# The first four slots of a per-sample matrix product with a residual, done with one row per partition

## Chip, cores and metric

The kernel runs on one core of a Trainium2 chip. The metric is the time of one execution on the device in microseconds (us), as the median of several runs.

## The reference

Each of 128 samples x[b] (128 rows c, 1024 columns t, float32) is multiplied by one of eight 128 x 128 matrices, which a list of subjects chooses, and added to itself:

```
w   = weights[subjects]                    # (128, 128, 128), subjects in 0..7
out = x + einsum("bct,bcd->bdt", x, w)     # x, out: (128, 128, 1024) float32
```

64 MB are read and 64 MB written. The residual costs no step of its own, since the kernel adds the identity to each matrix and multiplies once.

## The kernel before

**Slots.** A slot is four samples (Q = 4) and there are NT = 32 of them. The input buffer `x_in` holds IN = 4 slots, the output buffer `x_out` OUT = 8. A slot is 2 MiB each way. The two pairs of a slot (P = 2) have an accumulator each in PSUM, `ps[0]` and `ps[1]`, of four banks of 512 columns.

**Layout.** `load(k, p)` (L144) brings the two samples of pair p as one transfer of 1 MiB: sample h lies in partitions 64h to 64h+63, and each partition holds two neighbouring rows of it, 8 KB in one piece. `store` (L156) writes in the same way, 8 KB a run, 2 MiB a slot; the last twelve slots are stored in pairs of 4 MiB. With two rows in a partition a product of one sample has 64 partitions, and its 128 terms are two accumulated steps. `multiply` (L187) therefore issues 32 products of 64x64 by 512 columns for a slot, which TensorE runs four side by side; a float32 product is two instructions of TensorE.

**Matrices.** The matrices land in `w_raw` as they are, row c in partition c (L248). For the layout above row c has to stand in partition c/2, in both halves. Four products with the selection matrix `pick` move the rows (L296, into `ps[0]`), and two copies named `sort` write them in order to `w_all` (L231): half r = 1 on ScalarE (L305), half r = 0 on VectorE (L337). From `w_all`, `place` (L175) makes a slot's four matrices on VectorE: it picks the matrix by a subject read into a register, adds the identity `same`, and writes it to `ws[u]`, u alternating between slots.

**Order on the engines.** The order is written out by hand, and semaphores join the engines.

- ScalarE first issues the transfers of pair (0, 0), of the matrices, and of the other seven pairs (L247 to L290). Then it does its `sort`, and from then on for each slot `take` (L236): four copies `swap` (L225) move `ps[1]`, whose halves come out exchanged, to `x_out`. After each it waits for `s_eaten` and issues the two loads of the slot four further on.
- TensorE does idle products of zeros (IDLE = 6, L259), moves the rows (L296), and then runs `multiply` for one slot after another. A slot's product waits for `s_go` (its matrices are placed), `s_ready` (its input has landed) and `s_free` (the accumulator's half has been copied out).
- VectorE computes the subjects' indices, does its `sort`, waits for both sorts (`s_sort`), and places slots 0 and 1. Then for each slot it copies `ps[0]` to `x_out` in two halves of 1024 columns (L219), and places the matrices of the slot two further on. The first placing reports the slot to the store (`s_added[0]`), the second frees its input (`s_eaten`), the fourth gives `s_go`.
- GpSimd makes `pick` and `same`, and hands on landings (`s_ready`) and room in `x_out` (`s_room`, after a store has landed) in the order of the slots.
- SyncE issues a slot's store once VectorE and ScalarE have both reported it (L329).

`w_raw`, `pick`, `zeros` and the index scratch lie in the parts of `x_out` that belong to slots 6 and 7.

Of the kernel before, what the change touches and what calls it, by code (L numbers as in the profile page):

```python
# [27 lines left out]
ALU = mybir.AluOpType  # L28


H = 2

P = 2

R = 2

N = 512

IN = 4

OUT = 8
# [3 lines left out]

DMA = 16

IDLE = 6

ROWS = 8  # L50

ALIGN = 4096
QUEUES = {mybir.EngineType.SP: "qSPDynamicHW", mybir.EngineType.Activation: "qActDynamicHW"}
# [2 lines left out]
def transfer(nc, engine, out, in_):  # L56

    later, nc._always_lower_symbolic_ap = nc._always_lower_symbolic_ap, False  # L60
    ins, outs = engine.lower_ap_dma(in_), engine.lower_ap_dma(out)
    nc._always_lower_symbolic_ap = later
    return engine.add_instruction(
        mybir.InstDMACopy(
            name=nc.get_next_instruction_name(),
            engine=engine.engine,
            ins=ins,
            outs=outs,
            mode="Copy",
            cce_op=ALU.bypass,  # L70
            queue=QUEUES[engine.engine],
        )
    )
# [3 lines left out]
def kernel(  # L77
# [7 lines left out]
    nc = tc.nc  # L85
    B, C, T = x.shape
# [15 lines left out]
    if room:  # L102
# [4 lines left out]
    ws += [[sbuf(f"w{u}{p}", C, 1, R * D) for p in range(P)] for u in range(1, 2)]  # L107
    w_raw = x_out[:, (OUT * P - 1) * SIZE : (OUT * P - 1) * SIZE + S * D]
    pick = x_out[:, (OUT * P - 1) * SIZE + S * D :].rearrange("c (r p) -> c r p", p=C)[:, :R]
    zeros = x_out[:, (OUT * P - 2) * SIZE : (OUT * P - 2) * SIZE + N]  # L110
    given, near, wrap = (
        x_out[:1, (OUT * P - 3) * SIZE + k * B : (OUT * P - 3) * SIZE + (k + 1) * B].bitcast(I32)
        for k in range(3)
# [8 lines left out]
    s_zeros = tc.alloc_semaphore("s_zeros")  # L122
    s_same = tc.alloc_semaphore("s_same")
    s_pick = tc.alloc_semaphore("s_pick")
    s_picked = tc.alloc_semaphore("s_picked")
    s_sort = tc.alloc_semaphore("s_sort")
    s_ready = tc.alloc_semaphore("s_ready")
# [16 lines left out]
    def load(k, p, turn=None):  # L144
# [8 lines left out]
            x[bass.ds(first, H)].rearrange("h (b r) t -> (h b) (r t)", r=ROWS),  # L153
        ).then_inc(s_in[k % IN], DMA)

    def store(i, n):  # L156
        at = i % OUT * P * SIZE
        return transfer(
            nc,
            nc.sync,  # L160
            out[i * Q : (i + n) * Q].rearrange("(g h) (a r) t -> (h a) g (r t)", h=H, r=R),
            x_out[:, at : at + n * P * SIZE].rearrange("a (o f) -> a o f", o=1),
        )

# [10 lines left out]
    def place(u, subject):  # L175
        return [
            nc.vector.tensor_tensor(  # L177
                ws[u][p][h * A : (h + 1) * A],
                w_all[h * A : (h + 1) * A, bass.ds(subject[p * H + h], 1), :],
                same[h * A : (h + 1) * A],  # L180
                ALU.add,
            )
            for p in range(P)
            for h in range(H)
        ]

    def multiply(i):  # L187
        nc.tensor.wait_ge(s_go, 1).then_inc(s_go, -1)
# [28 lines left out]
    def copy(slot, half):  # L217
# [2 lines left out]
            x_out[:, bass.ds(at, T)], ps[0][:, banks].rearrange("d b n -> d (b n)")  # L220
        )

    def swap(slot, half, h):
        at, banks = half_of(slot, half)
        return nc.scalar.copy(  # L225
            x_out[h * A : (h + 1) * A, bass.ds(at + SIZE, T)],
            ps[1][(1 - h) * A : (2 - h) * A, banks].rearrange("d b n -> d (b n)"),
        )

    def sort(engine, r):  # L230
        engine(  # L231
            w_all.rearrange("c s (r e a) -> c r s e a", r=R, e=R)[:, r],
            ps[0][:, r * R : (r + 1) * R].rearrange("c g (s a e) -> c (g s) e a", a=A, e=R),
        ).then_inc(s_sort, 1)

    def take(i):  # L236
# [7 lines left out]

    with tc.tile_critical():  # L245

        load(0, 0)  # L247
        transfer(  # L248
            nc,
            nc.scalar,  # L250
            w_raw.rearrange("c (s d) -> c s d", s=S),
            weights.rearrange("s c d -> c s d"),
        ).then_inc(s_wall, DMA)
        nc.sync.dma_start(given, subjects.rearrange("(o b) -> o b", o=1)).then_inc(s_given, DMA)

        nc.vector.memset(zeros, 0.0).then_inc(s_zeros, 1)  # L256
        nc.tensor.wait_ge(s_zeros, 1)
        for _ in range(IDLE):
            nc.tensor.matmul(ps[P - 1][:, BANKS - 1], zeros[:, :D], zeros, start=True, stop=True)  # L259
        nc.vector.memset(index[:, B:], 0).then_inc(s_index, 1)  # L260

        nc.gpsimd.wait_ge(s_zeros, 1)
        nc.gpsimd.affine_select(  # L263
            pick.rearrange("c r (h b) -> c r h b", h=H),
            zeros[:, : R * C].rearrange("c (r h b) -> c r h b", r=R, h=H),
            [[-1, R], [0, H], [-R, A]],
            ALU.not_equal,
            1.0,
            base=0,
            channel_multiplier=1,  # L270
        ).then_inc(s_pick, 1)
# [12 lines left out]
        for p in range(P):  # L284
            nc.gpsimd.wait_ge(s_same, H).then_inc(s_room[p], OUT)

        for k in range(IN):
            for p in range(P):
                if (k, p) != (0, 0):
                    load(k, p)  # L290

        nc.tensor.wait_ge(s_pick, 1)
        nc.tensor.wait_ge(s_wall, DMA)
        for r in range(R):
            for g in range(S * D // N):
                nc.tensor.matmul(  # L296
                    ps[0][:, r * R + g],
                    pick[:, r],
                    w_raw[:, g * N : (g + 1) * N],
                    start=True,  # L300
                    stop=True,
                ).then_inc(s_picked, 1)

        nc.scalar.wait_ge(s_picked, S * D // N * R)
        sort(nc.scalar.copy, 1)  # L305
        with nc.scalar.Fori(0, NT // IN - 1) as turn:
            for k in range(IN):
                take((turn * IN + k) % OUT)
                nc.scalar.wait_ge(s_eaten, 1).then_inc(s_eaten, -1)
                for p in range(P):  # L310
                    load(IN + k, p, turn)
        for i in range(NT - IN, NT):
            take(i)

        nc.vector.wait_ge(s_given, DMA)
        nc.vector.tensor_scalar(near, given, -S, S - 1, ALU.max, ALU.min).then_inc(s_index, 1)  # L316
        nc.vector.wait_ge(s_index, 2)
        nc.vector.tensor_scalar(wrap, near, 0, S, ALU.is_lt, ALU.mult).then_inc(s_index, 1)  # L318
        nc.vector.wait_ge(s_index, 3)
        nc.vector.tensor_tensor(index[:, :B], near, wrap, ALU.add).then_inc(s_index, 1)  # L320

        for i in range(NT):
            if i - OUT in stored:
# [3 lines left out]
            nc.gpsimd.wait_ge(s_in[i % IN], DMA * P * (i // IN + 1)).then_inc(s_ready, 1)  # L327
# [12 lines left out]
        for u in range(2):  # L340
            placed = place(u, subject[u * Q : (u + 1) * Q])
            placed[0].then_inc(s_free[0], 1)
            placed[1].then_inc(s_free[1], 2)
            placed[-1].then_inc(s_go, 1)
        with nc.vector.Fori(0, NT // 2) as turn:  # L345
            for u in range(2):
                subject = subjects_of(bass.ds(turn * (2 * Q) + (u + 2) * Q, Q))
                slot = (turn * 2 + u) % OUT
                nc.vector.wait_ge(s_room[0], 1).then_inc(s_room[0], -1)
                for half in range(2):  # L350
                    nc.vector.wait_ge(s_product[0], H).then_inc(s_product[0], -H)  # L351
                    copied = copy(slot, half).then_inc(s_free[0], 1)
                placed = place(u, subject)
                placed[0].then_inc(s_added[0], 1)
                placed[1].then_inc(s_eaten, 1)
                placed[-1].then_inc(s_go, 1)
        with nc.tensor.Fori(0, NT // IN):
            for i in range(IN):
                multiply(i)

# [39 lines left out]
```

## Time and profile before

| | |
|---|---|
| median of 3 runs | 332.59 us (331.64 to 333.23) |
| profiled execution, whole time | 332.71 us |
| its span, first to last instruction | 330.9 us |
| moved by DMA | 134.81 MB, mean 407 GB/s over the span |
| TensorE, products | 255.5 us busy (77%) |
| VectorE | 138.0 us busy (42%) |
| ScalarE | 137.2 us busy (41%) |
| GpSimd | 1.6 us busy |
| mean granted TensorE clock | 0.928 |

The span is that of one profiled execution, and 1.8 us of its whole time lie around it. A busy share is a mean over the whole span. Where the work has stages with different limits, the rows by slices and stretches say more; in them a DMA packet is counted in the stretch in which it starts.

### The profile page before, as it was taken

The page shows a single profiled execution, that of the slowest core. Times are in us where ns is not written, and L with a number is a line of the kernel's source. Part 1 is how long each engine was busy: PE and PEld are TensorE (multiplying, and loading weights), DVE is VectorE, ACT ScalarE, POOL GpSimd, SP SyncE. Part 2 cuts the span into 40 slices and gives each one's busy share as a digit, 9 for nine tenths or more (in the row PEclk, how much of TensorE's full clock was granted, in tenths as well). Part 3 has the DMA queues.
Part 4 walks back from the last instruction along what each step waited for, and adds up shares of the span by engine and source line. Part 5 has one row for each costly group of instructions (what it writes and reads, how often), then busy time and mean ns, then how long its engine had stood idle before and what let it go on. Part 6 is the DMA issues. An engine that isn't in the chain of part 4 may idle for free. (4 is left out here: it accounts for less than half of the span.)

```text
span 330.9 us, 5722 instructions
## 1 busy us (share of the span) xinstructions
PE 255.5 (77%) x2068; PEld 93.3 (28%) x2068; DVE 138.0 (42%) x207; ACT 137.2 (41%) x162; POOL 1.6 (0%) x7
## 2 busy tenths in 40 slices
PE   7598888888888888888875897759887736999300
PEld 3243333333333333333222332213332302333100
DVE  1325555555444555555524255143555140444400
ACT  1105555555555555555525355153555050555500
POOL 1000000000000000000000000000000000000000
PEclk9979999999999999999979899798999775999955
DMA  7984999999999999999999999999999999999991
GB/s 277 428 372 129 431 421 416 436 432 426 442 418 434 436 424 434 444 428 426 430 442 402 434 424 435 428 428 430 432 450 424 430 432 436 428 408 432 436 440 48
DMA packets 7863, 134.81 MB, mean 407 GB/s; under 512 B 1457, under 2 KB 2482, under 8 KB 2482
## 3 DMA queue, kind: packets, MB, share of 16 engines
q10 hardware_dynamic: 4112, 67.64, 48.4%
q1 hardware_dynamic: 3746, 67.11, 47.5%
q8 instruction: 2, 0.03, 0.0%
q14 instruction: 3, 0.02, 0.0%
HBM read 67.63 MB, written 67.11 MB: 407 GB/s over the span
## 5 line engine op out<-in xcount | busy, mean ns | idle before, releaser
L202 PE MATMUL ps<-x_in,w 64*64 64x512 f32 x2048 | 244.2, 619 | 51.8 <-PEq L193 49.0
L225 ACT COPY x_out<-ps 64x1024 f32 (+1 forms) x128 | 128.8, 1007 | 161.9 <-ACTq L240 159.5
L202 PEld LDWEIGHTS ps<-x_in,w 64*64 64x64 f32 x2048 | 88.6, 138 | 207.3 <-issue 207.3
L219 DVE COPY x_out<-ps 128x1024 f32 x64 | 78.4, 1224 | 158.8 <-DVEq L351 158.8
L177 DVE TENSOR_TENSOR w<-w_all,same 64x256 f32<-64x256 f32 x136 | 57.1, 420 | 3.7
L259 PE MATMUL ps<-x_out 128*128 128x512 f32 x12 | 7.9, 825 | 1.7 <-DVE x_out L256 1.7
L243 ACT COPY mark<-same 1x1 f32 (+1 forms) x32 | 6.1, 190 | 0.8
L231 DVE COPY w_all<-ps 128x1024 f32<-128x1024 f32 x1 | 1.2, 1224 | 10.0 <-PE ps L296 10.0
L259 PEld LDWEIGHTS ps<-x_out 128*128 128x128 f32 x12 | 3.1, 270 | 5.6 <-issue 4.0
L231 ACT ACT_TABLE_LOAD x1 | 1.3, 1283 | 6.8 <-issue 6.8
L296 PE MATMUL ps<-x_out 128*128 128x512 f32 x8 | 3.6, 592 | 0.0
L231 ACT COPY w_all<-ps 128x1024 f32<-128x1024 f32 x1 | 1.0, 1012 | 4.9 <-PE ps L296 4.9
L296 PEld LDWEIGHTS ps<-x_out 128*128 128x128 f32 x8 | 1.5, 190 | 1.9 <-issue 1.9
L256 DVE MEMSET x_out<- 128x512 f32 x1 | 0.5, 485 | 1.0 <-SPq L245 1.0
L275 POOL TENSOR_SCALAR_AFFINE_SELECT same<-same 128x256 f32<-128x256 f32 x1 | 0.5, 529 | 0.1
L275 POOL TENSOR_SCALAR_AFFINE_SELECT same<-x_out 128x256 f32<-128x256 f32 x1 | 0.5, 479 | 0.0
L316 DVE TENSOR_SCALAR x_out<-x_out 1x128 int32<-1x128 int32 x1 | 0.2, 215 | 0.6 <-DMA x_out<-in_itok_B_dram 0.6
L263 POOL TENSOR_SCALAR_AFFINE_SELECT x_out<-x_out 128x256 f32<-128x256 f32 x1 | 0.4, 422 | 1.4 <-DVE x_out L256 1.4
L318 DVE TENSOR_SCALAR x_out<-x_out 1x128 int32<-1x128 int32 x1 | 0.3, 324 | 0.0
L320 DVE CUSTOM_DVE_ANT_0 index<-x_out 1x256 uint16<-1x256 uint16 x1 | 0.3, 279 | 0.0
L387 POOL MEMSET const-bfloat16-1.0<- 128x1 bf16 x1 | 0.1, 101 | 0.0
L387 POOL MEMSET const-uint8-127<- 128x1 uint8 x1 | 0.1, 101 | 0.0
(4 smaller groups left out, 0.3 us busy)
## 6 DMA issues: line engine op xcount, KB each, us to landing
x_in<-in_x_dram ACTq DMA_DIRECT2D x64, 1024.0 KB, 12.0
out_dram<-x_out SPq DMA_DIRECT2D x20, 2048.0 KB, 54.9
out_dram<-x_out SPq DMA_DIRECT2D x6, 4096.0 KB, 45.7
x_out<-in_L_cond_weights_dram ACTq DMA_DIRECT2D x1, 512.0 KB, 6.1
x_out<-in_itok_B_dram SPq DMA_DIRECT2D x1, 0.5 KB
```

The lines of the kernel that those rows point to most:

```text
L177: nc.vector.tensor_tensor(ws[u][p][h * A : (h + 1) * A], w_all[h * A : (h + 1) * A, bass.ds(subject[p * H + h], 1), :], same[h * A : (h + ...
L202: mm = nc.tensor.matmul(ps[p][cols, bank], ws[i % 2][p][rows, 0, r * D + e * A : r * D + (e + 1) * A], x_in[rows, at : at + N], start=r == ...
L219: return nc.vector.tensor_copy(x_out[:, bass.ds(at, T)], ps[0][:, banks].rearrange("d b n -> d (b n)"))
L225: return nc.scalar.copy(x_out[h * A : (h + 1) * A, bass.ds(at + SIZE, T)], ps[1][(1 - h) * A : (2 - h) * A, banks].rearrange("d b n -> d ( ...
L231: engine(w_all.rearrange("c s (r e a) -> c r s e a", r=R, e=R)[:, r], ps[0][:, r * R : (r + 1) * R].rearrange("c g (s a e) -> c (g s) e a" ...
L243: nc.scalar.copy(mark[:, bass.ds(slot, 1)], same[:1, 0, :1]).then_inc(s_added[1], 1)
L256: nc.vector.memset(zeros, 0.0).then_inc(s_zeros, 1)
L259: nc.tensor.matmul(ps[P - 1][:, BANKS - 1], zeros[:, :D], zeros, start=True, stop=True)
L263: nc.gpsimd.affine_select(pick.rearrange("c r (h b) -> c r h b", h=H), zeros[:, : R * C].rearrange("c (r h b) -> c r h b", r=R, h=H), [[-1 ...
L275: nc.gpsimd.affine_select(same[:, 0, :], same[:, 0, :] if h else zeros[:, : R * D], [[2 * C, R], [-2 * C, R], [-1, A]], ALU.not_equal, 1.0 ...
L296: nc.tensor.matmul(ps[0][:, r * R + g], pick[:, r], w_raw[:, g * N : (g + 1) * N], start=True, stop=True,).then_inc(s_picked, 1)
L318: nc.vector.tensor_scalar(wrap, near, 0, S, ALU.is_lt, ALU.mult).then_inc(s_index, 1)
```

## The change

Slots 0 to 3 (FIRST = 4) use another layout. `load_rows` brings one sample a transfer (512 KiB, sixteen transfers for the four slots) with row c in partition c, 4 KB in one piece, and the store of these slots writes rows of 4 KB. `place_rows` adds an identity `eye` (made on GpSimd ahead of `pick`) to a matrix as it landed in `w_raw`, 128 x 128. `multiply_rows` issues eight products of 128x128 by 512 columns for a slot, without accumulation, four into each accumulator, and reports each accumulator when its four are done. `copy_rows` on VectorE copies both accumulators, 2048 columns each, so that ScalarE has no part in these slots. Slots 4 to 31 go as before.

The rows are still moved for the later slots, ahead of slot 0, but into `ps[1]` instead of `ps[0]`. VectorE places slot 0 before its `sort`, and slot 1 after both sorts, with which `ps[1]` becomes free. Of the idle products three are left.

```diff
-IDLE = 6
+IDLE = 3
+FIRST = 4
...
+    def load_rows(i, q):
+        at = (i % IN * Q + q) * T
+        transfer(
+            nc,
+            nc.scalar,
+            x_in[:, at : at + T],
+            x[i * Q + q].rearrange("(b r) t -> b (r t)", r=C // 32),
+        ).then_inc(s_in[i % IN], DMA)
...
     def store(i, n):
         at = i % OUT * P * SIZE
+        if i < FIRST:
+            there = out[i * Q : (i + n) * Q].rearrange("g d t -> d g t")
+        else:
+            there = out[i * Q : (i + n) * Q].rearrange("(g h) (a r) t -> (h a) g (r t)", h=H, r=R)
...
+    def place_rows(u, subject):
+        return [
+            nc.vector.tensor_tensor(
+                ws[u][q // H][:, :, q % H * D : (q % H + 1) * D],
+                w_nat[:, bass.ds(subject[q], 1), :],
+                eye,
+                ALU.add,
+            )
+            for q in range(Q)
+        ]
+
+    def multiply_rows(slot, u):
+        nc.tensor.wait_ge(s_go, 1).then_inc(s_go, -1)
+        nc.tensor.wait_ge(s_ready, 1).then_inc(s_ready, -1)
+        for p in range(P):
+            nc.tensor.wait_ge(s_free[p], 1).then_inc(s_free[p], -1)
+            for bank in range(BANKS):
+                h, t = divmod(bank * N, T)
+                mm = nc.tensor.matmul(
+                    ps[p][:, bank],
+                    ws[u][p][:, 0, h * D : (h + 1) * D],
+                    x_in[:, bass.ds(slot * (Q * T) + ((p * H + h) * T + t), N)],
+                    start=True,
+                    stop=True,
+                )
+            mm.then_inc(s_product[p], 1)
...
+    def copy_rows(i, p):
+        at = i % OUT * P * SIZE + p * SIZE
+        return nc.vector.tensor_copy(
+            x_out[:, at : at + SIZE], ps[p].rearrange("d b n -> d (b n)")
+        )
...
-            ps[0][:, r * R : (r + 1) * R].rearrange("c g (s a e) -> c (g s) e a", a=A, e=R),
+            ps[1][:, r * R : (r + 1) * R].rearrange("c g (s a e) -> c (g s) e a", a=A, e=R),
         ).then_inc(s_sort, 1)
...
-        load(0, 0)
+        for q in range(H):
+            load_rows(0, q)
...
-        for k in range(IN):
-            for p in range(P):
-                if (k, p) != (0, 0):
-                    load(k, p)
+        for q in range(H, FIRST * Q):
+            load_rows(q // Q, q % Q)
...
         sort(nc.scalar.copy, 1)
-        with nc.scalar.Fori(0, NT // IN - 1) as turn:
+        for k in range(FIRST):
+            nc.scalar.wait_ge(s_eaten, 1).then_inc(s_eaten, -1)
+            for p in range(P):
+                load(FIRST + k, p)
+        with nc.scalar.Fori(0, (NT - FIRST) // IN - 1) as turn:
...
         for i, n in stores[:-1]:
-            for p in range(P):
-                nc.sync.wait_ge(s_added[p], i + n)
+            nc.sync.wait_ge(s_added[0], i + n)
+            if i >= FIRST:
+                nc.sync.wait_ge(s_added[1], i + n - FIRST)
...
         subject = subjects_of(slice(0, 2 * Q))
+        nc.vector.wait_ge(s_eye, 1)
+        nc.vector.wait_ge(s_wall, DMA)
+        placed = place_rows(0, subject[:Q])
+        placed[0].then_inc(s_free[0], 1)
+        placed[-1].then_inc(s_go, 1)
         nc.vector.wait_ge(s_picked, S * D // N * R)
         sort(nc.vector.tensor_copy, 0)
         nc.vector.wait_ge(s_sort, R)
+        placed = place_rows(1, subject[Q:])
+        placed[0].then_inc(s_free[1], 1)
+        placed[-1].then_inc(s_go, 1)
         nc.vector.wait_ge(s_same, H)
...
+        for i in range(FIRST):
+            subject = subjects_of(slice((i + 2) * Q, (i + 3) * Q))
+            nc.vector.wait_ge(s_room[0], 1).then_inc(s_room[0], -1)
+            for p in range(P):
+                nc.vector.wait_ge(s_product[p], 1).then_inc(s_product[p], -1)
+                copy_rows(i, p).then_inc(s_free[p], 1 if i < FIRST - 1 else R * (1 + p))
+            signal((place_rows if i + 2 < FIRST else place)(i % 2, subject))
...
+        with nc.tensor.Fori(0, FIRST // 2) as turn:
+            for u in range(2):
+                multiply_rows(turn * 2 + u, u)
```

What stands where on three engines follows, with the line numbers of each file. On TensorE, at the start of the program, before: idle products, row move, then the loop of `multiply`.

```order
L259 MATMUL ps<-x_out 128x512 x6
L296 MATMUL ps<-x_out 128x512 x4
L63 UNCONDITIONAL_BRANCH
L357 UNCONDITIONAL_BRANCH
L202 MATMUL ps<-x_in,w 64x512 x128
```

The same place in the changed kernel, where L225 is `multiply_rows`; the pair of its two rows stands sixteen times, for two slots.

```order
L313 MATMUL ps<-x_out 128x512 x3
L357 MATMUL ps<-x_out 128x512 x4
L65 UNCONDITIONAL_BRANCH
L437 UNCONDITIONAL_BRANCH
L225 ISA
L225 MATMUL ps<-x_in,w 128x512
```

The row move stays ahead of the first slot; three idle products are gone, and the first products are those of full height.

On VectorE, from the reading of the subjects to the first copies, before: the sorting copy (L231), then the placing (L177), which stands eight times.

```order
L166 TENSOR_LOAD index
L231 COPY w_all<-ps 128x8x128
L177 ISA
L177 TENSOR_TENSOR w<-w_all,same 64x256
```

In the changed kernel, where L209 is `place_rows` (four pairs at each place) and L284 the sorting copy:

```order
L186 TENSOR_LOAD index
L209 ISA
L209 TENSOR_TENSOR w<-x_out 128x128
...
L284 COPY w_all<-ps 128x8x128
L209 ISA
L209 TENSOR_TENSOR w<-x_out 128x128
...
L186 TENSOR_LOAD index
L272 COPY x_out<-ps 128x2048 x2
```

The placing of slot 0 has moved ahead of the sorting copy, and that of slot 1 stands behind it; a slot's copies are two of 2048 columns.

On ScalarE, from the first transfer to the first work on a slot, before (L63 issues transfers, L225 is `swap`):

```order
L63 DMA x_in<-in_x_dram 128x2048
L63 DMA x_out<-in_L_cond_weights_dram 128x8x128
L63 DMA x_in<-in_x_dram 128x2048 x7
L231 ACT_TABLE_LOAD
L231 COPY w_all<-ps 128x8x128
L306 UNCONDITIONAL_BRANCH
L225 ISA
L225 COPY x_out<-ps 64x1024
```

In the changed kernel (L65 issues transfers):

```order
L65 DMA x_in<-in_x_dram 128x1024 x2
L65 DMA x_out<-in_L_cond_weights_dram 128x8x128
L65 DMA x_in<-in_x_dram 128x1024 x14
L284 ACT_TABLE_LOAD
L284 COPY w_all<-ps 128x8x128
L65 DMA x_in<-in_x_dram 128x2048 x8
L371 UNCONDITIONAL_BRANCH
L278 ISA
```

The table load and the sorting copy now stand behind seventeen issues instead of nine, and the reloads of slots 4 to 7 are issued without a copy of ScalarE before them.

More of the change, by code (lines that the diff above doesn't have):

```diff
@@ L109 @@
     pick = x_out[:, (OUT * P - 1) * SIZE + S * D :].rearrange("c (r p) -> c r p", p=C)[:, :R]
+    w_nat = w_raw.rearrange("c (s d) -> c s d", s=S)
     zeros = x_out[:, (OUT * P - 2) * SIZE : (OUT * P - 2) * SIZE + N]
+    eye = x_out[:, (OUT * P - 2) * SIZE + N : (OUT * P - 2) * SIZE + N + D].rearrange(
+        "c (o d) -> c o d", o=1
+    )
     given, near, wrap = (
@@ L124 @@
     s_pick = tc.alloc_semaphore("s_pick")
+    s_eye = tc.alloc_semaphore("s_eye")
     s_picked = tc.alloc_semaphore("s_picked")
@@ L160, in store @@
             nc.sync,
-            out[i * Q : (i + n) * Q].rearrange("(g h) (a r) t -> (h a) g (r t)", h=H, r=R),
+            there,
             x_out[:, at : at + n * P * SIZE].rearrange("a (o f) -> a o f", o=1),
@@ L262 @@
         nc.gpsimd.wait_ge(s_zeros, 1)
+        nc.gpsimd.affine_select(
+            eye[:, 0],
+            zeros[:, :D],
+            [[-1, D]],
+            ALU.not_equal,
+            1.0,
+            base=0,
+            channel_multiplier=1,
+        ).then_inc(s_eye, 1)
         nc.gpsimd.affine_select(
@@ L296 @@
                 nc.tensor.matmul(
-                    ps[0][:, r * R + g],
+                    ps[1][:, r * R + g],
                     pick[:, r],
@@ L305 @@
         sort(nc.scalar.copy, 1)
-        with nc.scalar.Fori(0, NT // IN - 1) as turn:
+        for k in range(FIRST):
[3 more added lines that the diff above has]
+        with nc.scalar.Fori(0, (NT - FIRST) // IN - 1) as turn:
             for k in range(IN):
-                take((turn * IN + k) % OUT)
+                take((turn * IN + (FIRST + k)) % OUT)
                 nc.scalar.wait_ge(s_eaten, 1).then_inc(s_eaten, -1)
                 for p in range(P):
-                    load(IN + k, p, turn)
+                    load(FIRST + IN + k, p, turn)
         for i in range(NT - IN, NT):
@@ L326 @@
                     nc.gpsimd.wait_ge(s_out[i % OUT], count).then_inc(s_room[p], n)
-            nc.gpsimd.wait_ge(s_in[i % IN], DMA * P * (i // IN + 1)).then_inc(s_ready, 1)
+            landed = DMA * (Q + P * (i // IN))
+            nc.gpsimd.wait_ge(s_in[i % IN], landed).then_inc(s_ready, 1)
         for i, n in stores[:-1]:
-            for p in range(P):
-                nc.sync.wait_ge(s_added[p], i + n)
+            nc.sync.wait_ge(s_added[0], i + n)
+            if i >= FIRST:
+                nc.sync.wait_ge(s_added[1], i + n - FIRST)
             store(i, n).then_inc(s_out[i % OUT], DMA)
@@ L338, with signal @@
         nc.vector.wait_ge(s_sort, R)
+        placed = place_rows(1, subject[Q:])
+        placed[0].then_inc(s_free[1], 1)
+        placed[-1].then_inc(s_go, 1)
         nc.vector.wait_ge(s_same, H)
[L340 to L343, printed above, removed]
+        def signal(placed):
+            placed[0].then_inc(s_added[0], 1)
+            placed[1].then_inc(s_eaten, 1)
             placed[-1].then_inc(s_go, 1)
-        with nc.vector.Fori(0, NT // 2) as turn:
+        for i in range(FIRST):
[5 more added lines that the diff above has]
+            signal((place_rows if i + 2 < FIRST else place)(i % 2, subject))
+        with nc.vector.Fori(0, (NT - FIRST) // 2) as turn:
             for u in range(2):
-                subject = subjects_of(bass.ds(turn * (2 * Q) + (u + 2) * Q, Q))
-                slot = (turn * 2 + u) % OUT
+                subject = subjects_of(bass.ds(turn * (2 * Q) + (u + FIRST + 2) * Q, Q))
+                slot = (turn * 2 + (u + FIRST)) % OUT
                 nc.vector.wait_ge(s_room[0], 1).then_inc(s_room[0], -1)
@@ L352 @@
                     copied = copy(slot, half).then_inc(s_free[0], 1)
[L353 to L357, printed above, removed]
+                signal(place(u, subject))
+        with nc.tensor.Fori(0, FIRST // 2) as turn:
+            for u in range(2):
+                multiply_rows(turn * 2 + u, u)
+        with nc.tensor.Fori(0, (NT - FIRST) // IN):
             for i in range(IN):
```

3 lines of the change are left out of this document (2 added, 1 removed).

## Prediction

> **What bounds the kernel now.** I read the page first, and in it the span and the bandwidth row of the 40 slices.
>
> ```profile
> span 330.9 us, 5722 instructions
> PE 255.5 (77%) x2068; PEld 93.3 (28%) x2068; DVE 138.0 (42%) x207; ACT 137.2 (41%) x162; POOL 1.6 (0%) x7
> GB/s 277 428 372 129 431 421 416 436 432 426 442 418 434 436 424 434 444 428 426 430 442 402 434 424 435 428 428 430 432 450 424 430 432 436 428 408 432 436 440 48
> ```
>
> A slice is 330.9/40 = 8.27 us. From the fifth slice to the last but one the transfers run at about 430 GB/s throughout. TensorE is busy for 77% of the span, VectorE and ScalarE for about 42%, so no engine is full. The exceptions are the first slice, slices three and four (372 and 129), and the last. Slices three and four together lack 8.27 x (430-372 + 430-129)/430 = 6.9 us of transfer time. Next the table by stretches shows where that lies. Its last three columns are the granted clock, the busy share of the 16 DMA engines and GB/s; a packet counts in the stretch in which it starts, so a share can pass 1.
>
> ```profile
> 22.00:24.00 2.00, 2.00 (x24) 0.84 (x20) 0.00 (x0) 0.00 (x0) 0.00 (x0) 1.00 0.61 262
> 24.00:26.00 2.00, 1.57 (x16) 0.36 (x8) 1.33 (x2) 1.85 (x2) 0.00 (x0) 1.00 0.00 0
> 26.00:28.00 2.00, 1.69 (x16) 0.60 (x16) 1.94 (x3) 1.95 (x3) 0.00 (x0) 1.00 0.00 0
> 28.00:30.00 2.00, 1.88 (x20) 0.78 (x20) 0.86 (x3) 0.42 (x2) 0.00 (x0) 1.00 0.49 106
> 31.00:313.00 282.00, 230.81 (x1948) 83.51 (x1940) 127.98 (x186) 130.72 (x155) 0.00 (x0) 0.95 1.00 428
> ```
>
> The four slots' worth of input that fits in the buffers has been fetched by about 24 us, and nothing has been handed back or written: the DMA engines stand still for 2 x 0.39 + 4 + 2 x 0.51 = 5.8 us. After that they are full from 31 to 313 us (share 1.00). So every byte costs its share of 428 GB/s wherever it is moved, and the one thing to gain in the first third is that hole. A slot needs 2 x 2.10 MB / 0.430 = 9.8 us of transfer; TensorE's pace is shorter.
>
> ```profile
> 42.65 7.44 PE L202 MATMUL ps<-x_in,w 64*64 64x512 f32 x64 [0.72 <-PEq L193]
> 50.82 7.44 PE L202 MATMUL ps<-x_in,w 64*64 64x512 f32 x64 [0.73 <-PEq L193]
> ```
>
> That is 8.17 us a slot, so the engines matter only where the transfers run out of work. The way to the first store, which ends the hole, is in the timeline (start, duration, engine, line):
>
> ```profile
> 0.90 0.55 ACTq L63 DMA_DIRECT2D x_in<-in_x_dram  x1
> 1.48 0.66 ACTq L63 DMA_DIRECT2D x_out<-in_L_cond_weights_dram  x1
> 1.67 7.91 PE L259 MATMUL ps<-x_out 128*128 128x512 f32 x12 [1.67 <-DVE x_out L256]
> 1.85 0.42 POOL L263 TENSOR_SCALAR_AFFINE_SELECT x_out<-x_out 128x256 f32<-128x256 f32 x1 [1.41 <-DVE x_out L256]
> 2.17 4.65 ACTq L63 DMA_DIRECT2D x_in<-in_x_dram  x7
> 3.54 0.33 PEld L259 LDWEIGHTS ps<-x_out 128*128 128x128 f32 x1 [0.52 <-issue]
> 4.39 0.33 PEld L259 LDWEIGHTS ps<-x_out 128*128 128x128 f32 x1 [0.52 <-issue]
> 6.85 1.28 ACT L231 ACT_TABLE_LOAD   x1 [6.85 <-issue]
> 9.41 3.60 PE L296 MATMUL ps<-x_out 128*128 128x512 f32 x8
> 13.05 1.01 ACT L231 COPY w_all<-ps 128x1024 f32<-128x1024 f32 x1 [4.92 <-PE ps L296]
> 14.42 3.54 DVE L177 TENSOR_TENSOR w<-w_all,same 64x256 f32<-64x256 f32 x8
> 16.78 8.79 PE L202 MATMUL ps<-x_in,w 64*64 64x512 f32 x64 [3.77 <-PEq L193]
> 28.23 0.49 ACTq L63 DMA_DIRECT2D x_in<-in_x_dram  x1
> 28.54 33.20 SPq L63 DMA_DIRECT2D out_dram<-x_out  x5
> ```
>
> Before, slot 0's product follows warm-up, row move, sorting and placing one after another and starts at 16.78; the first reload is issued at 28.23 and the first store at 28.54 (a row that merges five stores up to 62 us).
>
> **The change part by part.** It gets slot 0 to its product without sorted weights. I follow three engines to the first store, with these durations beside the timeline's:
>
> ```profile
> L219 DVE COPY x_out<-ps 128x1024 f32 x64 | 78.4, 1224 | 158.8 <-DVEq L351 158.8
> L177 DVE TENSOR_TENSOR w<-w_all,same 64x256 f32<-64x256 f32 x136 | 57.1, 420 | 3.7
> x_out<-in_L_cond_weights_dram ACTq DMA_DIRECT2D x1, 512.0 KB, 6.1
> L166 DVEq TENSOR_LOAD <-index x33: 345/560/1156, 3.1 to 302.0; - x33
> ```
>
> TensorE: a cold 512-column instruction takes 4.39 - 3.54 = 0.85 us, a warm one 3.60/8 = 0.45. The warm-up shrinks from 12 instructions to 6, so it ends at 1.67 + 6 x 0.85 = 6.8 instead of 9.6. The matrices landed at 1.48 + 6.1 = 7.6; the same 1.5 MB stand ahead of that point in the queue, so I keep 7.6. The row move starts there, 1.8 us earlier than its 9.41, and ends at 11.2. Slot 0 needs four row loads, which with the matrices are the first 2.6 MB: moving from about 2.1 (1.2 us behind the first issue, a lag shown below) at 0.43 MB/us, they are through near 8.3 and landed by 10, covered by the row move. Four whole matrices are placed straight from the landed ones: between 1224 ns for 1024 columns and 420 ns for 256 lies 1.05 ns a column, so 128 columns take 0.29, with the gaps of 3.54/8 - 0.42 about 0.31; four end at 7.6 + 1.2 = 8.8, also under the row move. The added selection on GpSimd puts the one that the row move needs back by at most 0.42, from an end at 2.3 to 2.7; 7.6 covers it. The first half of slot 0 (8 instructions, 3.6 us at 0.45) runs from 11.2 to 14.8; it uses ps0, the row move now ps1, so it need not wait for the sorting.
>
> ScalarE: 17 DMAs of which 16 are half as large, instead of 9. Issue takes 0.55 to 0.66 each (4.65/7), so they end at 0.9 + 0.58 + 16 x 0.66 = 12.0 instead of 6.8. The queue is still fed ahead: half a megabyte takes 1.2 us to move. But the table load (1.28) and the sorting copy (1.01) now end at 14.3, behind the issue and not behind the row move. VectorE waits for that copy before it places slot 1's matrices, whose first frees ps1 at 14.6. So slot 0's second half is not held: 14.8 to 18.4. ScalarE's next wait is the one for slot 0's end, and behind it are queued only the reloads that need that end anyway.
>
> VectorE's new waits, for the selection and the landed matrices, hold back only its sorting copy, which needs the row move's end anyway. After the sorting: four placings to 15.6, a register load of 0.56, then two copies of 2048 columns, each 1.22 + 1.07 = 2.3: 16.2 to 18.5, and, the product being there at 18.4, 18.5 to 20.8. The first placing of slot 2 signals the store at 21.1, the second the reload at 21.4. With hand-over, the store is issued at about 21.2 (28.54 before) and the reload at 21.5 (28.23).
>
> What that is worth: in the profile the reload of 28.23 gives its first packets after 29, about 1.2 us behind. The new store and reload flow from 22.5 on, and the input loads end near 24. The margin is 1.5 us, so the whole hole of 5.8 us closes. No second hole opens: 4.2 MB from slot 0 fill 9.8 us, to 33.8, and slot 1 follows one slot pace (about 7 us) behind slot 0, near 28. What is late next is nothing on an engine: the transfers are then full from 3 us to the end. All other edits (ScalarE free of four slots' swaps, the 128 x 128 products, two VectorE copies in place of one plus four swaps) lie under full transfers and are put at nothing; without that cover the slower of TensorE and VectorE would set about 7 us a slot, still below 8.17.
>
> An added cost: 4 KB runs replace 8 KB runs in 16.8 MB. The nearest row with small runs is the fetch of the matrices in 512-byte packets (GpSimd's busy time, clock, share, GB/s):
>
> ```profile
> 5.50:6.00 0.50, 0.00 (x0) 1.00 0.97 290
> ```
>
> 290/0.97 = 299 GB/s of full engines against 430: 27.4 ns a packet instead of 19.0, so at most 8.4 ns a run. 2048 more runs on 16 engines are 1.1 us. The lower bound is 0, since the 8 KB runs show full rate; 4 KB is nearer to 8 KB than to 512 bytes, so I take 0.3 us.
>
> Sum for the profiled execution, 332.7 us (span 330.9 and 1.8 around it): 332.7 - 5.8 + 0.3 = 327.2. It stands 0.1 above the median of the runs, 332.6, so the forecast is 327.1 us, 1.7% less.
>
> **The rivals.** *The first store comes late.* The clock rows speak for it:
>
> ```profile
> 16.00:18.00 2.00, 1.22 (x8) 0.56 (x12) 1.86 (x5) 0.00 (x0) 0.00 (x0) 0.74 0.88 377
> 18.00:20.00 2.00, 2.00 (x12) 0.64 (x8) 0.00 (x0) 0.00 (x0) 0.00 (x0) 0.50 0.95 410
> ```
>
> After 3.77 us without a product the clock fell to 0.50. And the warm-up was slow to lift it: of its 12 instructions c were cold with 0.85 c + 0.45 (12 - c) = 7.91, so c is about 6, and the new warm-up of 6 ends just where the clock rose. If it does not rise, the row move takes 8 x 0.85 = 6.8 us and ends at 14.4, slot 0 at 21.6, its copy at 23.9, and the store issued at 24.3 flows at 25.5, 1.5 us after the loads end: 328.6. ScalarE can cause the same: if the queue took a DMA only every 1.2 us once nine are in flight, issue would end near 14.4, the store would be some 2.3 us later and the hole about 0.8. Against it: up to 6.8 us TensorE does what it did before, and the row move resumes work after 0.8 us. I give this family 0.15. [...]
>
> *The gain is given back at the end.* The last chain is slots 28 to 31, then a store of 4 MB:
>
> ```profile
> 275.86 9.02 PE L202 MATMUL ps<-x_in,w 64*64 64x512 f32 x64 [8.47 <-PEq L193]
> 312.60 0.54 SPq L63 DMA_DIRECT2D out_dram<-x_out  x1
> 305.00:310.00 5.00, 3.98 (x40) 1.36 (x32) 1.93 (x2) 2.58 (x3) 0.00 (x0) 1.00 1.04 446
> 310.00:315.00 5.00, 0.00 (x0) 0.00 (x0) 2.20 (x5) 1.64 (x3) 0.00 (x0) 0.89 0.95 406
> 323.00:324.00 1.00, 0.00 (x0) 0.00 (x0) 0.00 (x0) 0.00 (x0) 0.00 (x0) 0.50 0.23 98
> ```
>
> The earlier stores are just drained when the last is issued (0.95), and its 4.2 MB end at 323 (share 0.23). If slot 28 did not start earlier, the engines would idle there and nothing would be won: 332.6. Against it: TensorE waits 8.47 us before slot 28, and what it waits for is room in x_out or input, both of which come with transfers that all lie 5.8 us earlier. Chance 0.07.
>
> *Slower: the 4 KB runs do not run at full rate.* Place: the loads and stores of slots 0 to 3. At the 299 GB/s of the 512-byte row, 16.8 MB take 56.1 us instead of 39.0: 332.6 - 5.8 + 17.1 = 343.9. It decides from below 16.8/(39.0 + 5.8) = 375 GB/s. Against it: a run is eight times that packet, and the bound above is 1.1 us if the cost is one per run. Chance 0.05. [...]
>
> **How the numbers follow.** Forecast 0.73, late store 0.15, given back 0.07, slower 0.05. The low end is the forecast with the 6.9 us of the slices and no cost of runs, 325.7; measuring spreads by some 0.2%, so 325.5. The high end is the late store with the whole 1.1 us of the runs: 332.6 - 5.8 + 1.5 + 1.1 = 329.4, rounded to 329.6. The two other cases lie outside. What a measurement can tell from no change is about 0.5%, 1.7 us: faster 0.88, same 0.07, slower 0.05.
>
> **What would show it.** Right: slices three and four at about 430 GB/s; row move from 7.6 to about 11.2; the sorting copy of ScalarE ending near 14.3; first store issued near 21.2; no zero stretch after 3 us; everything later as before, only 5 to 6 us earlier. Wrong: a zero stretch left near 24 (late store); a DMA share of 1 at clearly under 430 GB/s before 45 us (runs); a share under 1 between 270 and 315 us (given back at the end).

## The result, and the profile after

| | before | changed | ratio (95% interval) |
|---|---|---|---|
| median | 332.56 us (331.64 to 333.23, 4 runs) | 328.28 us (327.83 to 328.75, 4 runs) | 0.9873 (0.9845 to 0.9902) |
| span of the profiled execution | 330.9 us | 326.8 us | |

The kernel is faster by 1.3%, 4.3 us; 5.5 us (327.1) were forecast, with a range of 325.5 to 329.6. From the page of the changed kernel, the span, the bandwidth by slices (8.17 us each) and the two data queues (packets, MB, share of 16 engines over the span):

```profile
span 326.8 us, 5288 instructions
GB/s 238 424 415 311 434 423 433 428 419 441 423 435 429 429 431 427 435 427 429 427 439 427 419 450 441 425 417 415 453 419 439 437 413 429 449 429 409 441 445 40
q10 hardware_dynamic: 4496, 67.64, 49.1%
q1 hardware_dynamic: 3746, 67.11, 48.3%
```

The same two queue rows of the kernel before:

```profile
q10 hardware_dynamic: 4112, 67.64, 48.4%
q1 hardware_dynamic: 3746, 67.11, 47.5%
```

Slices three and four, 372 and 129 before, are now 415 and 311: most of the hole is filled, not all. The queue rows give the balance. Before, the packets filled (48.4 + 47.5)% of 330.9 = 317.3 us and the engines stood still for 13.6; now they fill 97.4% of 326.8 = 318.3 and stand still for 8.5. So 5.1 us of standing were won and 1.0 us of transfer time was added. The shares are rounded to 0.1%, so each of these two differences is uncertain by some 0.5 us. By stretches (columns as in the prediction):

```profile
22.00:24.00 2.00, 2.00 (x6) 0.95 (x5) 2.00 (x3) 0.00 (x0) 0.00 (x0) 1.00 1.01 426
24.00:26.00 2.00, 2.00 (x6) 0.86 (x5) 1.66 (x4) 0.00 (x0) 0.00 (x0) 1.00 0.74 311
26.00:28.00 2.00, 2.00 (x6) 0.84 (x5) 1.21 (x1) 0.00 (x0) 0.00 (x0) 1.00 1.11 303
28.00:30.00 2.00, 2.00 (x6) 0.95 (x5) 1.65 (x1) 0.00 (x0) 0.00 (x0) 1.00 1.04 295
31.00:313.00 282.00, 224.40 (x1818) 82.05 (x1816) 128.49 (x183) 117.98 (x140) 0.00 (x0) 0.95 1.00 429
```

Of the 5.8 us of pause a dent is left, 2 x 0.26 = 0.5 us. Behind it the engines are full but move only about 300 GB/s for some 4 us. From 31 us to 313 us the rate is as before. The way to the first store:

```profile
1.67 5.13 PE L313 MATMUL ps<-x_out 128*128 128x512 f32 x6 [1.67 <-DVE x_out L310]
2.12 0.66 ACTq L65 DMA_DIRECT2D x_out<-in_L_cond_weights_dram  x1
9.10 5.37 PE L357 MATMUL ps<-x_out 128*128 128x512 f32 x8 [2.30 <-DMA x_out<-in_L_cond_weights_dram]
12.90 1.28 ACT L284 ACT_TABLE_LOAD   x1 [12.90 <-issue]
14.30 27.63 PE L225 MATMUL ps<-x_in,w 128*128 x64
14.51 1.01 ACT L284 COPY w_all<-ps 128x1024 f32<-128x1024 f32 x1 [0.33 <-PE ps L357]
18.06 2.29 DVE L272 COPY x_out<-ps 128x2048 f32<-128x2048 f32 x1 [1.28 <-DVEq L425]
21.48 2.29 DVE L272 COPY x_out<-ps 128x2048 f32<-128x2048 f32 x1 [1.13 <-DVEq L425]
24.00 0.64 SPq L65 DMA_DIRECT2D out_dram<-x_out  x1
24.29 1.26 ACTq L65 DMA_DIRECT2D x_in<-in_x_dram  x2
```

The first store is issued at 24.00, 4.5 us earlier than before but 2.8 later than forecast. The row move waits until 9.1 for the matrices and then takes 5.37 us instead of 3.60; from there on the chain goes as forecast, on TensorE and VectorE without a gap of more than 1.3 us. The late landing shows in the first of these stretches, where the packets in flight move only 200 GB/s (341 in the same stretch before; why is not shown), and the reason for the 5.37 is the clock in the others (third column from the end):

```profile
4.00:6.00 2.00, 2.00 (x3) 0.67 (x2) 0.00 (x0) 0.00 (x0) 0.00 (x0) 1.00 0.62 200
...
8.00:10.00 2.00, 0.90 (x2) 0.51 (x3) 0.81 (x4) 0.00 (x0) 0.00 (x0) 0.93 1.09 453
10.00:12.00 2.00, 2.00 (x3) 0.67 (x2) 0.09 (x1) 0.00 (x0) 0.00 (x0) 0.50 0.92 393
12.00:14.00 2.00, 2.00 (x5) 0.96 (x4) 0.00 (x0) 1.10 (x1) 0.00 (x0) 0.72 1.04 442
```

### The profile page after: what moved, and what is told of

Same layout as the page of the kernel before. It is cut to its first block, busy times and chain, and to the rows that moved or that the text cites. A ratio compares the mean times of both kernels' runs of the same rounds, so it can differ in the third digit from the quotient of the medians.

```text
span 326.8 us, 5288 instructions
## 1 busy us (share of the span) xinstructions
PE 251.4 (77%) x1870; PEld 93.5 (29%) x1870; DVE 143.4 (44%) x207; ACT 120.3 (37%) x142; POOL 1.8 (1%) x8
## 3 DMA queue, kind: packets, MB, share of 16 engines
q10 hardware_dynamic: 4496, 67.64, 49.1%
q1 hardware_dynamic: 3746, 67.11, 48.3%
## 5 line engine op out<-in xcount | busy, mean ns | idle before, releaser
L249 PE MATMUL ps<-x_in,w 64*64 64x512 f32 x1792 | 213.5, 619 | 49.6 <-PEq L240 47.5
L278 ACT COPY x_out<-ps 64x1024 f32 (+1 forms) x112 | 112.6, 1006 | 173.5 <-ACTq L293 167.5
L266 DVE COPY x_out<-ps 128x1024 f32 x56 | 68.6, 1224 | 143.6 <-DVEq L434 143.6
L249 PEld LDWEIGHTS ps<-x_in,w 64*64 64x64 f32 x1792 | 77.5, 138 | 185.5 <-issue 185.5
L197 DVE TENSOR_TENSOR w<-w_all,same 64x256 f32<-64x256 f32 x120 | 50.4, 420 | 3.2
L225 PE MATMUL ps<-x_in,w 128*128 x64 | 27.6, 592 | 0.0
L272 DVE COPY x_out<-ps 128x2048 f32<-128x2048 f32 x8 | 18.3, 2291 | 6.0 <-DVEq L425 6.0
L225 PEld LDWEIGHTS ps<-x_in,w 128*128 128x128 f32 x64 | 12.2, 190 | 15.3 <-issue 15.3
L357 PE MATMUL ps<-x_out 128*128 128x512 f32 x8 | 5.4, 836 | 2.3 <-DMA x_out<-in_L_cond_weights_dram 2.3
L313 PE MATMUL ps<-x_out 128*128 128x512 f32 x6 | 5.1, 1028 | 1.7 <-DVE x_out L310 1.7
L209 DVE TENSOR_TENSOR w<-x_out 128x128 f32<-128x128 f32 x16 | 3.6, 285 | 6.1 <-DMA x_out<-in_L_cond_weights_dram 5.9
L284 ACT ACT_TABLE_LOAD x1 | 1.3, 1283 | 12.9 <-issue 12.9
L284 DVE COPY w_all<-ps 128x1024 f32<-128x1024 f32 x1 | 1.2, 1225 | 4.4 <-PE ps L357 4.4
L284 ACT COPY w_all<-ps 128x1024 f32<-128x1024 f32 x1 | 1.0, 1012 | 0.3 <-PE ps L357 0.3
## 6 DMA issues: line engine op xcount, KB each, us to landing
x_in<-in_x_dram ACTq DMA_DIRECT2D x56, 1024.0 KB, 14.3
```

Of the source, the lines that this page charges most:

```text
L197: nc.vector.tensor_tensor(ws[u][p][h * A : (h + 1) * A], w_all[h * A : (h + 1) * A, bass.ds(subject[p * H + h], 1), :], same[h * A : (h + ...
L209: nc.vector.tensor_tensor(ws[u][q // H][:, :, q % H * D : (q % H + 1) * D], w_nat[:, bass.ds(subject[q], 1), :], eye, ALU.add,)
L225: mm = nc.tensor.matmul(ps[p][:, bank], ws[u][p][:, 0, h * D : (h + 1) * D], x_in[:, bass.ds(slot * (Q * T) + ((p * H + h) * T + t), N)], ...
L249: mm = nc.tensor.matmul(ps[p][cols, bank], ws[i % 2][p][rows, 0, r * D + e * A : r * D + (e + 1) * A], x_in[rows, at : at + N], start=r == ...
L266: return nc.vector.tensor_copy(x_out[:, bass.ds(at, T)], ps[0][:, banks].rearrange("d b n -> d (b n)"))
L272: return nc.vector.tensor_copy(x_out[:, at : at + SIZE], ps[p].rearrange("d b n -> d (b n)"))
```

## The experiments

**Theory.** Time is transfer work plus the time in which the DMA engines stand still, and the only pause that can be moved is the one before the first store and reload; each us of it costs one. **Rival of less work:** the gain is in the wide products and in ScalarE's missing copies. **On the shortfall:** the late row move on one side, the 4 KB runs on the other. For each kernel one row of the stretch from 20 to 36 us is shown, whose last two columns are the DMA share and GB/s; what it lacks of 430 is 16 x (430 - GB/s)/430 us. In that stretch before has

```profile
20.00:36.00 16.00, 14.42 (x132) 5.41 (x124) 7.22 (x10) 7.84 (x9) 0.00 (x0) 0.99 0.62 232
```

which lacks 7.4 us, and the changed kernel has

```profile
20.00:36.00 16.00, 16.00 (x39) 7.11 (x38) 11.90 (x14) 0.00 (x0) 0.00 (x0) 1.00 1.01 380
```

which lacks 1.9.

**1. Everything of the change, but late.**

```diff
-IDLE = 3
+IDLE = 13
```

> The changed kernel with 13 idle products instead of 3 (26 instructions of TensorE), so that the row move starts near 15.4 us and the first store is issued near 28.5 us, as before the change. All else is the changed kernel: row layout, wide products, ScalarE free in four slots, 4 KB runs. Theory of the hole (the gain is the transfer time won because the first store and reload come earlier): the stretch without transfers is back at about 5 us and the time is 332.5 to 333.5. Rival of less work (the gain comes from the wide products, from ScalarE's missing copies or from other transfers, wherever the first store lies): it stays below 330.

Measured: 333.59 us, ratio to before 1.002 (1.0005 to 1.0036). The expectation of 332.5 to 333.5 was missed by 0.1. The first store and the stretch:

```profile
27.94 0.64 SPq L65 DMA_DIRECT2D out_dram<-x_out  x1
```

```profile
20.00:36.00 16.00, 16.00 (x39) 7.15 (x38) 11.78 (x17) 0.00 (x0) 0.00 (x0) 1.00 0.75 267
```

With the wide products, the free ScalarE and the 4 KB runs all in place, nothing is left of the gain once the first store comes about as late as before. The rival of less work falls. The fit is not perfect: the stretch lacks 6.1 us, 1.3 less than before, and yet the median lies 0.8 above the 332.79 of before that was measured beside it. The first 20 us take 0.8 of those 1.3 back (last table of this section); the rest is not explained.

**2. Old layout, earlier order.** In the kernel before:

```diff
-IDLE = 6
+IDLE = 3
...
-        load(0, 0)
         transfer(
             nc,
             nc.scalar,
             w_raw.rearrange("c (s d) -> c s d", s=S),
             weights.rearrange("s c d -> c s d"),
         ).then_inc(s_wall, DMA)
+        load(0, 0)
```

> The kernel before, in its old layout for all slots, with two edits of order alone: the transfer of the matrices is issued ahead of the first input, and 3 idle products instead of 6, so that the row move starts near 6.8 us instead of 9.4. No wide products, no 4 KB runs. Theory of the hole: the first store is issued at 24.3 to 25.7 instead of 28.5, and the time falls by about as much, to 329 to 330. Rival of less work: without the new layout nothing is gained, 332.6.

Measured: 330.17 us, ratio 0.9936 (0.9911 to 0.996), a little above the 329 to 330 expected.

```profile
25.68 0.62 SPq L63 DMA_DIRECT2D out_dram<-x_out  x1
```

```profile
20.00:36.00 16.00, 14.29 (x132) 5.10 (x128) 8.26 (x12) 8.43 (x10) 0.00 (x0) 1.00 0.81 311
```

The store comes 2.9 us earlier, the stretch lacks 4.4 us instead of 7.4, and the time falls by 2.6 against before measured beside it (332.79). About half of what the change brings (0.64% of 1.27%) is to be had without the new layout.

**3. TensorE kept at work until the matrices land.**

```diff
-IDLE = 3
+IDLE = 5
```

> The changed kernel with 5 idle products instead of 3, so that TensorE works from 1.7 to about 8.5 us and idles only 0.6 us until the matrices land near 9.1. Theory that the late first store of the changed kernel (24.0 instead of the 21.2 predicted) comes in part from a cold row move: the row move takes 3.6 us instead of 5.4 and ends near 12.7, the first store is issued at 22.3 to 23.0, the remaining dent of 0.6 us near 25 us goes, and the time falls by 0.3 to 0.7 us to about 327.7. Rival (the clock does not matter, or ScalarE's sorting copy holds the first store just as late): first store within 0.5 us of 24.0, time unchanged at 328.3.

Measured: 326.58 us, ratio 0.9819 (0.9796 to 0.9842), just below the changed kernel's interval (0.9845 to 0.9902).

```profile
1.67 6.44 PE L313 MATMUL ps<-x_out 128*128 128x512 f32 x10 [1.67 <-DVE x_out L310]
8.56 3.67 PE L357 MATMUL ps<-x_out 128*128 128x512 f32 x8 [0.45 <-DMA x_out<-in_L_cond_weights_dram]
12.17 1.28 ACT L284 ACT_TABLE_LOAD   x1 [12.17 <-issue]
13.47 1.01 ACT L284 COPY w_all<-ps 128x1024 f32<-128x1024 f32 x1
21.77 7.41 SPq L65 DMA_DIRECT2D out_dram<-x_out  x2
```

```profile
20.00:36.00 16.00, 16.00 (x38) 7.03 (x37) 13.01 (x15) 0.00 (x0) 0.00 (x0) 1.00 0.99 405
```

The row move takes 3.67 us, the store comes at 21.77, the dent is gone (0.9 us lacking). The store is earlier than the 22.3 to 23.0 expected because the matrices also landed 0.5 us earlier here, at 8.56; that part is not the edit's doing. ScalarE's sorting copy ends at 14.48, where the prediction had put it (14.3), and does not hold the store. The gain over the changed kernel, 1.7 us, is larger than the 0.3 to 0.7 expected. In the two profiles 0.9 us of it lies in this stretch, where most of the slow transfers behind the dent went with it (410 GB/s from 26 to 28 us, where the changed kernel has 303); the rest lies in the first 20 us and at the end (last table of this section).

**4. The matrices first, in the row layout,** and beside it the changed kernel once more.

```diff
-        for q in range(H):
-            load_rows(0, q)
         transfer(
             nc,
             nc.scalar,
             w_raw.rearrange("c (s d) -> c s d", s=S),
             weights.rearrange("s c d -> c s d"),
         ).then_inc(s_wall, DMA)
+        for q in range(H):
+            load_rows(0, q)
```

> The changed kernel itself, once more, on the chip of the two kernels beside it, so that they can be compared with it: 328 to 328.6 us, first store issued near 24.0, a dent of about 0.6 us near 25 us.

Measured: 328.14 us, ratio 0.9859 (0.9836 to 0.9882). The time is as expected, the first store and the dent are not:

```profile
9.91 5.37 PE L357 MATMUL ps<-x_out 128*128 128x512 f32 x8 [2.76 <-DMA x_out<-in_L_cond_weights_dram]
24.82 7.41 SPq L65 DMA_DIRECT2D out_dram<-x_out  x2
```

```profile
20.00:36.00 16.00, 16.00 (x39) 7.06 (x38) 11.93 (x13) 0.00 (x0) 0.00 (x0) 1.00 0.94 354
```

In this execution of the same kernel the matrices landed 0.8 us later, at 9.91, the store came 0.8 us later, and the stretch lacks 2.8 us instead of 1.9. So a single profile of this kernel places its first store no better than to about 1 us.

> The changed kernel with one edit of order: the transfer of the matrices is issued ahead of the first two row loads. The matrices land near 5, so that the row move follows the three idle products without a pause, from 6.8 to 10.4 us, on a warm clock. Theory of the hole: the first store is issued near 21, the dent near 25 us goes, and the time falls to what the kernel with 5 idle products has, 326.6 within 0.5, and no lower, since nothing stands still any more. Rival (an earlier first store goes on paying): below 326.

Measured: 326.76 us, ratio 0.9824 (0.9798 to 0.985), 1.4 us below the changed kernel beside it; the two intervals overlap a little.

```profile
6.21 3.60 PE L357 MATMUL ps<-x_out 128*128 128x512 f32 x8
11.12 3.70 PE L225 MATMUL ps<-x_in,w 128*128 x8 [1.32 <-PEq L222]
21.45 7.41 SPq L65 DMA_DIRECT2D out_dram<-x_out  x2
```

```profile
20.00:36.00 16.00, 16.00 (x39) 7.12 (x38) 12.97 (x16) 0.00 (x0) 0.00 (x0) 1.00 1.01 418
```

A second way to the same store time gives the same time. **And sorting earlier still:**

```diff
+EARLY = 10
...
-        for q in range(H, FIRST * Q):
+        for q in range(EARLY):
             load_rows(q // Q, q % Q)
...
         sort(nc.scalar.copy, 1)
+        for q in range(EARLY, FIRST * Q):
+            load_rows(q // Q, q % Q)
```

> The same, and ScalarE does its sorting copy after 10 of the 16 row loads instead of after all of them. The first store comes another 1 us earlier, near 20. Theory of the hole: the transfers have no pause that this could fill, so the time is that of the kernel beside it with the matrices first, within 0.5 us. Rival (an earlier first store goes on paying): 1 us less.

Measured: 326.87 us, ratio 0.9828 (0.9796 to 0.9861). The premise failed: the store is issued at 21.43, no earlier. Slot 0's product starts at 11.63 after a wait of 0.64 us. Beside it, in the kernel without this edit, it starts at 11.12 after 1.32 us. Its matrices were placed by 6.8, so what it waits for is its own input. Beside it, the second half of slot 0 also waited 0.26 us for the sorting copy; the later start takes back what the earlier copy saves:

```profile
11.63 23.87 PE L227 MATMUL ps<-x_in,w 128*128 x55 [0.64 <-PEq L224]
21.43 7.41 SPq L67 DMA_DIRECT2D out_dram<-x_out  x2
```

The stretch from 20 to 36 us lacks nothing here:

```profile
20.00:36.00 16.00, 16.00 (x39) 7.11 (x38) 12.98 (x16) 0.00 (x0) 0.00 (x0) 1.00 1.02 435
```

So whether a store before 21.4 would bring anything was not tried. The equal times of experiments 3 and 4 only agree with the theory there.

**5. Twice as many 4 KB runs.** FIRST = 8, the row loads of slots 4 to 7 issued in place of their reloads, TensorE's loop of `multiply_rows` run twice, and the counts of `s_in` and `s_room` that follow from it (the diff shows the loads alone).

```diff
-FIRST = 4
+FIRST = 8
...
-        for q in range(H, FIRST * Q):
+        for q in range(H, IN * Q):
             load_rows(q // Q, q % Q)
...
-            for p in range(P):
-                load(FIRST + k, p)
+            if IN + k < FIRST:
+                for q in range(Q):
+                    load_rows(IN + k, q)
+            else:
+                for p in range(P):
+                    load(IN + k, p)
```

> The changed kernel with eight slots in the row layout instead of four, so twice as many 4 KB runs (33.6 MB of the 134.8). Theory that the 4 KB runs cost transfer time: the sum of the two data queues' shares times the span, which rose by about 1.0 us with four slots, rises by another 1.0 us, and the time goes to about 329.3. Rival (runs cost nothing, and the slow stretch from 26 to 32 us belongs to the first stores beside the first reloads, whatever their runs): the sum stays, the stretch looks the same, and the time stays at 328.3 within 0.4.

Measured: 327.2 us, ratio 0.983 (0.9808 to 0.9853), span 324.8.

```profile
q10 hardware_dynamic: 4880, 67.64, 49.3%
q1 hardware_dynamic: 3746, 67.11, 48.7%
```

```profile
20.00:36.00 16.00, 16.00 (x38) 7.03 (x37) 12.07 (x13) 0.00 (x0) 0.00 (x0) 1.00 1.01 392
```

The packets fill 98.0% of 324.8 = 318.3 us, as much as with four slots. Another 16.8 MB in 4 KB runs cost nothing that these rows show (their rounding is 0.3 us). The packets suggest why a price per run did not hold: with FIRST = 0, 4 and 8 the queue of the loads has 4112, 4496 and 4880, 384 more each time, and that of the stores 3746 in all three. That it was 1 us faster than the changed kernel was not expected; its stretch lacks 1.4 us instead of 1.9, its first store came 0.5 earlier, and the rest lies in the tail described at the end. It isn't explained further.

**All runs side by side.** Each column of lost time is worked out from one row of the profile, as what the stretch lacks of 430 GB/s; the last is counted from 315 us to the end of the span. From 36 to 315 us every kernel moves 428 to 431 GB/s.

| kernel | first store, us | lacks 0 to 20 | lacks 20 to 36 | lacks behind 315 | span of the profile | median |
|---|---|---|---|---|---|---|
| before | 28.54 | 2.9 | 7.4 | 6.9 | 330.9 | 332.56 |
| 1, late | 27.94 | 3.7 | 6.1 | 6.8 | 330.4 | 333.59 |
| 2, old layout, earlier order | 25.68 | 2.9 | 4.4 | 7.6 | 328.0 | 330.17 |
| changed | 24.00 | 3.8 | 1.9 | 7.5 | 326.8 | 328.28 |
| changed, again | 24.82 | 4.1 | 2.8 | 6.7 | 327.0 | 328.14 |
| 3, five idle products | 21.77 | 3.5 | 0.9 | 6.8 | 324.9 | 326.58 |
| 4, matrices first | 21.45 | 3.5 | 0.4 | 6.2 | 324.8 | 326.76 |
| 4, and early sorting | 21.43 | 4.1 | 0.0 | 8.8 | 327.0 | 326.87 |
| 5, eight slots | 23.49 | 3.9 | 1.4 | 5.5 | 324.8 | 327.20 |

What the stretch from 20 to 36 us lacks goes with the first store, and the medians follow it, experiment 1 apart. The seven profiles with row loads lose 0.6 to 1.2 us more in the first 20 us than the two without; what in the row loads does it was not tried. The end varies by 3.3 us from profile to profile and does not follow the edits, so differences of 1 us between two profiles prove little; for those the medians count.

## Why the prediction was right, point by point

- **What bounds it: right.** Transfers are full from 31 to 313 us in both kernels (share 1.00, 428 and 429 GB/s), and the time follows the first store. Before, experiment 2, the changed kernel and experiment 3 issue it at 28.5, 25.7, 24.0 and 21.8 us and take 332.6, 330.2, 328.3 and 326.6: 2.4 for 2.9, 1.9 for 1.7, 1.7 for 2.2. Experiment 1 lies some 1.5 us above such a line and experiment 5 some 0.7 below it, and the changed kernel's second profile has a store 0.8 us later at the same median. So "each us of it costs one" holds to 1 or 1.5 us.
- **The chain on TensorE: mis-sized.** "The matrices landed at 1.48 + 6.1 = 7.6 ... so I keep 7.6. The row move starts there ... and ends at 11.2." They landed at 9.1 (8.6 to 9.9 in the four other profiles of this order): their issue had moved from 1.48 to 2.12 behind two row loads, and then they took 7.0 us instead of 6.1, while the transfers of 4 to 6 us moved 200 GB/s. And after 2.3 us without a product, not 0.8, the clock fell to 0.50 and the row move took 5.4 us instead of 3.6. Together the row move ended 3.3 us later than forecast and the store 2.8.
- **The rival of the late store came true in its numbers, by another way.** It was given 0.15 and 328.6, with a clock that does not rise; the store came at 24.0 where it said 24.3. But the clock had risen (1.00 from 9.0 to 9.5 us, two weight loads in 0.30 us at 9.07) and fell soon after the longer wait (0.72 from 9.5 to 10.0 us, then 0.50, with 0.34 us for one load), and 1.5 of the 3.3 us are the late landing, which no rival had. That its time lies so near the measured one is in part luck. Its price was 1.5 us. The dent itself is 0.5, and experiment 3, which takes away the dent, the cold clock and most of the slow transfers, wins 1.7.
- **The chain on ScalarE: right within 0.9 us.** Seventeen issues end at 12.9 (12.0 forecast), table load and sorting copy follow, and the row move ended last anyway.
- **The hole: nearly right in size.** It was to close whole; 5.8 us shrank to 0.5, and to 1.2 in the second profile of the changed kernel.
- **The cost of runs: inside its bound, wrong in its cause.** 0.3 us was taken, with 1.1 as bound; 1.0 us of transfer time was added. But it does not go with the number of 4 KB runs (experiment 5). The busy share less GB/s over 430 gives 0.5 us more than before in the first 20 us, and 0.7 more from 20 to 36 us, in the slow transfers behind the dent; without the dent it shrinks: experiment 3 has (49.4 + 48.4)% of 324.9 = 317.8 us.
- **Given back at the end: did not happen.** Slot 28 starts 4.05 us earlier, at 271.81 instead of 275.86, with the same wait before it:

```profile
271.81 9.13 PE L249 MATMUL ps<-x_in,w 64*64 64x512 f32 x64 [8.52 <-PEq L240]
```

The sum as it came out: -5.3 for the hole and +1.0 of transfer time make -4.3; the span lost 4.1. The same by stretches shows a term that the prediction put at nothing, the start, with "the transfers are then full from 3 us to the end". First before, then the changed kernel:

```profile
0.00:20.00 20.00, 14.56 (x36) 5.84 (x40) 5.91 (x15) 2.29 (x2) 1.59 (x7) 0.92 0.90 367
0.00:20.00 20.00, 16.03 (x28) 6.65 (x29) 6.48 (x16) 2.29 (x2) 1.78 (x8) 0.91 0.88 348
```

The stretch from 20 to 36 us won 5.5 us, the first 20 us lost 0.9, and the end 0.5.

## What to carry to other kernels

Where transfers are full from some point to the end, look for the stretch before it in which they stand still, and price an edit by what it does to the first store and the first reload, not by the work it saves on engines. Ask of each early transfer what stands ahead of it in its queue: here, issuing the half megabyte that everything waits for first, or bridging the wait with two more idle products, was worth 0.4 to 0.6% on top of a change of 1.3%. Before a new layout, try the order: it gave 0.6% alone.

## What the runs showed of the hardware

- In the changed kernel the granted clock fell to 0.50 after a pause of 2.30 us in TensorE, and in three profiles with pauses of 2.25 to 2.76 us the row move behind them took 5.37 us. After 0.45 us (experiment 3) it took 3.67 us, and after 1.32 us (experiment 4) slot 0's first eight instructions took 3.70. The prediction had a fall only after 3.77 us.
- In three profiles the transfers ran slowly at full share soon behind their pause: the changed kernel at 295 to 303 GB/s from 26 to 30 us, the one of experiment 1 at 262 and 311 from 30 to 34 us, and in the old layout experiment 2 at 270 from 26 to 28 us (third line):

```profile
30.00:32.00 2.00, 2.00 (x6) 0.80 (x6) 1.15 (x1) 0.00 (x0) 0.00 (x0) 1.00 1.05 262
32.00:34.00 2.00, 2.00 (x6) 0.94 (x5) 1.71 (x1) 0.00 (x0) 0.00 (x0) 1.00 0.97 311
26.00:28.00 2.00, 2.00 (x24) 0.88 (x20) 0.05 (x1) 0.00 (x0) 0.00 (x0) 1.00 1.03 270
```

So it is not the 4 KB runs alone. Where no pause came before the first stores and reloads (experiment 4 with early sorting), the stretch from 20 to 36 us moved 435 GB/s. What slowed the transfers behind the pauses stays open.

- The last transfers did not end together: in the changed kernel the share is 0.81 from 315 to 320 us and 0.06, as much as one engine of sixteen, from 320 to 325. From 320 to 325 us the second profile of the changed kernel has 0.09, experiments 3 and 5 and both of experiment 4 have 0.03 to 0.06, and before has 0.05 from 325 to 330.

```profile
315.00:320.00 5.00, 0.00 (x0) 0.00 (x0) 0.00 (x0) 0.00 (x0) 0.00 (x0) 0.50 0.81 347
320.00:325.00 5.00, 0.00 (x0) 0.00 (x0) 0.00 (x0) 0.00 (x0) 0.00 (x0) 0.50 0.06 26
```

That tail of some 5 us is as large as the hole was; what held up the last transfers was not tried.
